# A decoder layer in float32: q and k of the first two head pairs by seven block products instead of direct projections

## The chip, the core and the metric

One core of a Trainium2 chip runs the whole program. The metric is the device time in microseconds (us) of one execution, as the median of several. TensorE is PE in the profile (PEld its weight loads), VectorE is DVE, ScalarE is ACT, GpSimd is POOL, and SP issues almost all DMAs, in the order in which they stand on its queue.

## The reference

A decoder layer over four batches of 1024 tokens and 512 features: attention, a gated causal convolution and a quantised feed-forward layer, each with a residual and a norm. The change concerns only the projections at the start. q, k and v are each two linear layers in a row:

```python
q = _lin(_lin(x, wq_w, wq_b), vq_w, vq_b)
k = _lin(_lin(x, wk_w, wk_b), vk_w, vk_b)
v = _lin(_lin(x, wv_w, wv_b), vv_w, vv_b)
...
scores = jnp.einsum('cbqh,cbkh->cbqk', q, k) / scale
attn = jax.nn.softmax(scores, axis=-1)
o = jnp.einsum('cbqk,cbkh->cbqh', attn, v)
```

There are 32 heads of 16 features. Everything is float32.

## The kernel before

**Set-up.** The two weights of each projection are multiplied once on TensorE ("fold", line 384 for q and k), so that q, k and v become one product each with x. The two biases are folded too: VectorE multiplies rows of the second weight by the first bias (line 367), reduces them (line 368) and adds the second bias (line 369). V's folded bias, `b_vc`, is a column over partitions but is needed as a row on all partitions, so it goes out to DRAM and comes back broadcast (lines 800 and 801). V's own fold (`fold_v`, line 546) is done in eight pieces of 256 columns.

**Units and pairs.** Attention runs in 32 units of four heads. A pair is two units of one batch and has 128 features of q and of k. The features of a pair are computed into a pack with 128 partitions, and `to_quadrants` (line 398) then moves 16 rows of each head to the start of a quadrant of 32 partitions, by four DMAs for each unit and each of q and k. Four units' worth of quadrants exist (`q_ts`, `k_ts`).

**Two ways to compute q and k.** `project` (line 407) computes one pair directly: six pieces of 176 or 160 columns, each four input tiles by four column groups of TensorE (`by_quarters`). It serves pairs 0 and 1. All later pairs are made two at a time by `product` (line 482): the two pairs and the two halves of the tokens form a 2 by 2 block matrix, the two halves of the input features another, and seven block products (in Winograd's form of Strassen's method) replace eight. The seven need sums of blocks of the weights (`sum_w`, four additions of 128 × 256 on POOL) and of x (`sums_of_x`, four of 128 × 1024 on POOL, of which the last overwrites one block of x). The result of each product is copied from PSUM by ScalarE and added to the right blocks by POOL; products 2, 3 and 4 go through one of four scratch rows ("rooms"). Product 7 uses `b_diff`, the difference of two pairs' biases.

**The order around the change** is written out by hand, engine by engine. Ahead of the first scores: two pieces of q of pair 0, then the other ten pieces of pair 0, with `to_quadrants` after q's last and after k's last, then five of V's eight folds, three sums of x, the sums of w for pair 2, and V's bias through DRAM. Then step u = −1 computes the row maxima of unit 0 (`nat`, line 603; half of them, "nats", use slots of the pool `ps_st`, which has four), and between groups of them a list of filling work: the last three folds, the 12 pieces of pair 1, V's block sums and the fourth sum of x, V's products for batch 0, and the first six parts of pairs 2 and 3. V's first products are added to `v_sb` by VectorE straight from PSUM, with V's bias row; V's later ones are copied by ScalarE to the rooms and added by POOL. x of batch 1 is loaded at the start of this step. After it the units of attention follow, always with the maxima of the next unit between the scores of this one.

Of the kernel before, what the change touches and what calls it, by code (L numbers as in the profile page):

```python
# [8 lines left out]
F32 = mybir.dt.float32  # L9
AF = mybir.ActivationFunctionType  # L10
ALU = mybir.AluOpType
# [41 lines left out]
def by_quarters(nc, pt, lhsT, rhs, tiles=FT):  # L53


    for f in range(tiles):
        for j in range(4):
            r = slice(32 * j, 32 * j + 32)
            nc.tensor.matmul(pt[r, :], lhsT(f)[:, r], rhs(f), start=f == 0, stop=f == tiles - 1)  # L59
# [193 lines left out]
def attention(ctx, tc, a, attn_d, ident, shared, hand):  # L253
# [7 lines left out]
    b_k = const.tile([P, FT], F32, tag="b_k", name="b_k")  # L261
    b_v = shared.tile([P, D], F32, tag="b_f", name="b_v")

    def big_slot(b, name):
        return shared.tile([P, NT * (D + 1)], F32, tag=f"big{b % 2}", name=name)

# [81 lines left out]
    for which, (w, v, dst) in enumerate((("wq", "vq", b_q), ("wk", "vk", b_k), ("wv", "vv", None))):  # L348
        w_n = sp.tile([P, FT, D], F32, tag="w_n", name=f"w_n{which}")
        v_t = sp.tile([P, FT, D], F32, tag="v_t", name=f"v_t{which}")  # L350
        for m in range(FT):
            rows = slice(m * P, (m + 1) * P)
            nc.sync.dma_start(w_n[:, m, :], a[f"{w}_w"][rows, :])

            (nc.scalar if which == 0 else nc.sync).dma_start(v_t[:, m, :], a[f"{v}_wT"][rows, :])
        v_n = w_v if which == 2 else rows_of_v[:, which * FT : (which + 1) * FT, :]
        w_b = sp.tile([P, D], F32, tag="w_b", name=f"w_b{which}")
        v_b = sp.tile([P, FT], F32, tag="v_bc", name=f"v_b{which}")
        if dst is None:
            dst = sp.tile([P, FT], F32, tag="b_vc", bufs=1, name="b_vc")  # L360

        def bias(w=w, v=v, dst=dst, v_n=v_n, w_b=w_b, v_b=v_b):

            nc.sync.dma_start(v_n, a[f"{v}_w"].rearrange("(t p) m -> p t m", p=P))
            nc.sync.dma_start(w_b, a[f"{w}_b"].partition_broadcast(P))
            nc.sync.dma_start(v_b, a[f"{v}_bc"])
            nc.vector.tensor_mul(v_n, v_n, w_b.unsqueeze(1).to_broadcast([P, FT, D]))
            nc.vector.tensor_reduce(dst, v_n, AX.X, ALU.add)
            nc.vector.tensor_add(dst, dst, v_b)

        if which == 2:
            bias()
            b_d = dpool.tile([D], F32, tag="b_v", bufs=1, name="b_vd")
            b_vc = dst
            break
        if which == 1:
            xts[0] = load_x(0)
        bias()
        w_d = (w_q, w_k)[which]

        pts = [ps.tile([P, D], F32, tag="ps", name=f"fold{which}_{f}") for f in range(FT)]
        for m in range(FT):
            for f in range(FT):
                nc.tensor.matmul(  # L384
                    pts[f], w_n[:, m, f * P : (f + 1) * P], v_t[:, m, :], start=m == 0, stop=m == FT - 1
                )
        for f in range(FT):
            if f % 2:
                nc.scalar.copy(w_d[:, f, :], pts[f])
            else:  # L390
                nc.vector.tensor_copy(w_d[:, f, :], pts[f])
# [6 lines left out]
    def to_quadrants(u, which, packed):  # L398
# [4 lines left out]
            nc.sync.dma_start(dst[32 * j : 32 * j + HD, :], packed[h * HD : (h + 1) * HD, :])  # L403
        if which == 0 and u >= 4:
            nc.sync.dma_start(dst[HD::32, :], dst[HD + 1 :: 32, :])

    def project(p, which, t0, n, packed, pool=None):

        b, gg = divmod(p, 4)
        w, bias = ((w_q, b_q), (w_k, b_k))[which]  # L410
        cols = slice(t0, t0 + n)
        pt = (pool or ps_st).tile([P, QW], F32, tag="ps" if pool else "st", name=f"proj{p}_{which}_{t0}")
        by_quarters(nc, pt[:, 0:n], lambda f: w[:, f, gg * P : (gg + 1) * P], lambda f: xts[b][:, f, cols])
        nc.scalar.activation(packed[:, cols], pt[:, 0:n], AF.Identity, bias=bias[:, gg : gg + 1], scale=1.0)
        if t0 + n == S:
            to_quadrants(2 * p, which, packed)
            to_quadrants(2 * p + 1, which, packed)

    def qk_pieces(p, which):

        parts = [(0, 176), (176, 176), (352, 176), (528, 176), (704, 160), (864, 160)]
        return [
            lambda pool=None, part=part: project(p, which, *part, packs[p][:, which, :], pool) for part in parts
        ]

# [51 lines left out]
        rooms.append(rooms.pop(0))  # L479
        return rooms[-1]  # L480

    def product(p, which, i, t0, n):

        b, gg = divmod(p, 4)
        left, right = operands(i, blocks_of_w(p, which), [w_sums[:, which, k, :, :] for k in range(4)], b)
        cols = slice(t0, t0 + n)
        pt = ps_st.tile([P, 512], F32, tag="st", name=f"part{i}_{p}_{which}_{t0}")[:, 0:n]
        by_quarters(nc, pt, lambda k: left[:, k, :], lambda k: right[:, k, cols], 2)
        c11, c12, c21, c22 = (
            packs[which][:, o, 512 * t + t0 : 512 * t + t0 + n] for o in range(2) for t in range(2)  # L490
        )
        if i in (2, 3, 4):
            dst = room()[:, 0:n]
        else:
            dst = {1: c11, 5: c22, 6: c12, 7: c21}[i]
        if i in (1, 7):
            bias = (b_q, b_k)[which][:, gg : gg + 1] if i == 1 else b_diff[:, which, gg // 2 : gg // 2 + 1]
            nc.scalar.activation(dst, pt, AF.Identity, bias=bias, scale=1.0)
        else:
            nc.scalar.copy(dst, pt)  # L500
        add = nc.gpsimd.tensor_add
        if i == 6:
            add(c12, c12, c11)
        elif i == 2:
            add(c11, c11, dst)
        elif i == 7:
            add(c21, c21, c12)
        elif i == 5:
            add(c12, c12, c22)
            add(c22, c22, c21)  # L510
        elif i == 3:
            add(c12, c12, dst)
        elif i == 4:
            nc.gpsimd.tensor_sub(c21, c21, dst)

    due = {}

    def products(p, which):


        rows = [(2 * p - 3, 2), (2 * p - 2, 2), (2 * p - 1, 2), (2 * p, 2)]
        if which == 1:
            rows = [(2 * p - 2, 22), (2 * p - 2, 26), (2 * p - 1, 4), (2 * p, 4)]
        for n, when in enumerate(rows):
            due.setdefault(when, []).append(lambda n=n: to_quadrants(2 * p + n, which, packs[which][:, n // 2, :]))
        return [
            [
                lambda part=part: product(p, which, *part)
                for part in parts
            ]  # L530
            for parts in (
                [(1, 0, 256), (1, 256, 256), (6, 0, 256), (6, 256, 256), (2, 0, 256), (2, 256, 256)],
                [(7, 0, 512), (5, 0, 512), (3, 0, 256), (3, 256, 256), (4, 0, 256), (4, 256, 256)],
            )
        ]


    early = qk_pieces(0, 0)
    for piece in early[:2]:
        piece(early_ps)  # L540
    setup_ps.close()

    ps_st = ctx.enter_context(tc.tile_pool(name="ps_st", bufs=4, space=PSUM))
# [243 lines left out]
    ]  # L787

    folds = [lambda f=f, half=half: fold_v(f, half) for f in range(FT) for half in range(2)]

    b_diff = const.tile([P, 2, 2], F32, tag="b_diff", name="b_diff")
    for which, bias in enumerate((b_q, b_k)):
        nc.vector.tensor_tensor(b_diff[:, which, :], bias[:, 1::2], bias[:, 0::2], ALU.subtract)
    for piece in early[2:] + qk_pieces(0, 1) + folds[:5]:
        piece()
    late_sum = sums_of_x(0)
    for work in late_sum[:3]:
        work()
    sum_w(2, 0)
    nc.sync.dma_start(b_d.rearrange("(t p) -> p t", p=P), b_vc)  # L800
    nc.sync.dma_start(b_v, b_d.partition_broadcast(P))

    for u in range(-1, NU):
        fill = []
# [12 lines left out]
        if u == -1:  # L817
            def sums():
                sum_blocks(v_blocks, v_sums)
                late_sum[3]()  # L820

            vs = v_parts[:6] + [[(i, t), (j, t)] for t in range(4) for i, j in ((6, 7), (5, 4))]
            fill = folds[5:] + qk_pieces(1, 0) + qk_pieces(1, 1) + [sums] + [
                lambda part=part: v_products(0, part) for part in vs
            ] + fill
        elif units[u][0] + 1 < B:
            b, g = units[u][0] + 1, units[u][1]
            v1, v2 = (lambda n=n, b=b: v_products(b, v_parts[n]) for n in (2 * g, 2 * g + 1))

            fill = {  # L830
                0: fill[:2] + [v1] + fill[2:4] + [v2] + fill[4:],
                1: [v1, v2] + fill,
                2: fill[:2] + [v1] + fill[2:4] + [v2] + fill[4:],
                3: fill + [v1, v2],
            }[w]
# [445 lines left out]
```

## Time and profile before

| what | us |
|---|---|
| median of 4 runs (2400.5 to 2401.67) | 2401.46 |
| the profiled execution, as timed | 2401.24 |
| its span, first to last instruction | 2399.3 |
| folds of q and k on TensorE | 5.48 to 33.38 |
| q and k of pair 0 | 33.38 to 47.30 |
| five of V's folds | 47.30 to 56.05 |
| first score product (maxima of unit 0) | 56.05 |
| first scores for the exponentials | 127.99 |

In the page, the first part gives busy times of the engines and their share of the span, and the fourth part the chain of work that ended last, followed back from the end. In a line of a timeline the first number is the start, the second the time taken (of a merged group: from its first start to its last end), then engine, line, operation, output from inputs, shape and number of records, and in brackets the idle time ahead of it and what ended it. A float32 matmul leaves two records. Matmuls overlap, so a group's time is read best from one start to the next.

### The profile page before, as it was taken

How to read it: one execution, taken by the hardware profiler on the slowest of the kernel's cores; microseconds unless marked ns; L12 is line 12 of the kernel's file. 1: busy time of each engine (PE TensorE's matmuls, PEld its weight loads, DVE VectorE, ACT ScalarE, POOL GpSimd, SP SyncE). 2: the span in 40 equal slices, each digit the busy share in tenths (PEclk: the TensorE clock that was granted, in tenths of full speed). 3: DMA queues.
4: the chain of work that ended last, by engine and by line, in shares of the span. 5: the costliest groups of instructions: out<-in, count | busy, mean ns of one | idle time of the engine just before them, and what ended most of it. 6: DMA issues, size and time to landing. Idle time of an engine off the chain costs nothing.

```text
span 2399.3 us, 70081 instructions
## 1 busy us (share of the span) xinstructions
PE 2391.9 (100%) x30124; PEld 1617.0 (67%) x30124; DVE 1724.3 (72%) x2153; ACT 1361.3 (57%) x2693; POOL 713.6 (30%) x728
## 2 busy tenths in 40 slices
PE   9999999999999999999999999999999999999999
PEld 6566666666666666666666666666666799747994
DVE  3667777777777777777777777777777477868678
ACT  1166666666666666666666666666666723411333
POOL 4332322212223322222322212211110268422761
PEclk9999999999999999999999999999999999999999
DMA  6200112011001110110111012202300242160311
GB/s 224 60 2 17 27 25 56 17 30 25 18 17 30 21 52 21 30 21 17 31 21 22 17 30 77 63 17 50 93 12 13 82 150 89 67 232 18 124 36 70
DMA packets 80838, 121.43 MB, mean 51 GB/s; under 512 B 39072, under 2 KB 39328, under 8 KB 80528
## 3 DMA queue, kind: packets, MB, share of 16 engines
q1 hardware_dynamic: 79808, 115.77, 17.1%
q8 instruction: 237, 3.88, 0.7%
q10 hardware_dynamic: 720, 1.18, 0.1%
q14 instruction: 73, 0.60, 0.1%
HBM read 80.77 MB, written 18.35 MB: 41 GB/s over the span
## 4 chain that ended last, share of the span: by engine, by line
PE 99%; POOL 0%; DVE 0%; ACT 0%; DMA 0%; issue 0%; SPq 0%; DVEq 0%; ACTq 0%; POOLq 0%
PE nat L616 22%; PE av L712 20%; PE st L686 19%; PE part L59 8%; PE pc L1018 6%; PE pa L1018 6%; PE pf L1102 5%; PE v L59 4%; PE po L59 2%; PE po L242 2%; PE proj L59 1%; PE fold L384 1%; PE tr L1094 1%; PE fold L59 1%; PE nats L616 0%; POOL v_sb L588 0%
## 5 line engine op out<-in xcount | busy, mean ns | idle before, releaser
L632 DVE TENSOR_REDUCE mx<-nat 128x2 f32<-128x1024 f32 x1008 | 1187.9, 1220 | 436.2 <-PE st L686 401.7
L697 ACT ACTIVATE at<-st 128x512 f32<-128x512 f32 x2016 | 1042.6, 602 | 477.7 <-PE st L686 467.6
L616 PE MATMUL nat<-qk 32*128 32x512 f32 x4032 | 1011.5, 614 | 0.5 <-DVE mx L632 0.5
L686 PE MATMUL st<-qk 32*128 32x256 f32 x8064 | 1001.6, 387 | 0.0
L686 PEld LDWEIGHTS st<-qk 32*128 32x128 f32 x8064 | 691.4, 184 | 43.2 <-issue 1.2
L712 PE MATMUL av<-at,v_sb 128*32 128x256 f32 x8192 | 497.7, 382 | 0.3 <-ACT at L697 0.3
L616 PEld LDWEIGHTS nat<-qk 32*128 32x128 f32 x4032 | 343.7, 184 | 220.5 <-DVE mx L632 134.1
L712 PEld LDWEIGHTS av<-at,v_sb 128*32 128x32 f32 x8192 | 241.5, 109 | 220.5 <-ACT at L697 88.4
L759 POOL TENSOR_TENSOR o_n<-o_sb,rbc 128x512 f32<-128x512 f32 x64 | 95.8, 1518 | 226.6 <-DMA rbc<-rec_d 150.1
L1018 PE MATMUL pa<-xf,w 128*128 128x171 f32 x1024 | 159.8, 308 | 0.0
L1018 PE MATMUL pc<-xf,w 128*128 128x171 f32 x1024 | 159.7, 308 | 0.0
L1018 PEld LDWEIGHTS pc<-xf,w 128*128 128x128 f32 x1024 | 152.0, 189 | 0.9 <-issue 0.9
L1018 PEld LDWEIGHTS pa<-xf,w 128*128 128x128 f32 x1024 | 152.0, 189 | 0.0
L1029 ACT ACTIVATE u<-u,b_c 128x512 f32<-128x512 f32 x64 | 46.1, 721 | 158.8 <-DVE u L1028 158.8
L1102 PE MATMUL pf<-w_f,xq_t 128*128 128x512 f32 (+1 forms) x264 | 114.8, 579 | 0.0
L171 POOL TENSOR_TENSOR w<-w 128x512 f32<-128x512 f32 x64 | 81.4, 1305 | 95.4 <-DMA w<-in_conv_wT 63.5
L725 DVE TENSOR_TENSOR o_sb<-av,o_sb 128x256 f32<-128x256 f32 x128 | 54.4, 425 | 68.3 <-PE av L712 67.8
L723 ACT COPY o_sb<-av 128x256 f32<-128x256 f32 x128 | 48.0, 375 | 77.7 <-PE av L712 64.5
L588 POOL TENSOR_TENSOR v_sb<-v_sb,extra 128x256 f32<-128x256 f32 x68 | 44.7, 686 | 139.7 <-ACT extra L572 139.7
L588 POOL TENSOR_TENSOR v_sb<-v_sb,rooms 128x256 f32<-128x256 f32 x56 | 36.8, 686 | 155.1 <-ACT rooms L572 155.1
L1102 PEld LDWEIGHTS pf<-w_f,xq_t 128*128 128x128 f32 x264 | 47.9, 190 | 45.8 <-issue 45.4
L1025 DVE SCALAR_TENSOR_TENSOR u<-pa,u 128x342 f32<-128x342 f32 x64 | 40.6, 635 | 50.5 <-PE pa L1018 48.0
(172 smaller groups left out, 2039.9 us busy)
## 6 DMA issues: line engine op xcount, KB each, us to landing
w<-in_conv_wT SPq DMA_DIRECT2D x32, 512.0 KB
u<-in_ctx SPq DMA_DIRECT2D x16, 1024.0 KB
xT<-in_xT SPq DMA_DIRECT2D x16, 512.0 KB
qk<-qk SPq DMA_DIRECT2D x128, 64.0 KB
qk<-extra SPq DMA_DIRECT2D x128, 64.0 KB
rbc<-rec_d SPq DMA_DIRECT2D x128, 64.0 KB
attn<-o_n SPq DMA_DIRECT2D x256, 32.0 KB
big<-attn SPq DMA_DIRECT2D x4, 2048.0 KB
```

Source lines behind the costliest of these rows:

```text
L59: nc.tensor.matmul(pt[r, :], lhsT(f)[:, r], rhs(f), start=f == 0, stop=f == tiles - 1)
L171: self.nc.gpsimd.tensor_tensor(w[:, i, tap, :], w[:, i, 0, :], w[:, i, 1, :], op)
L588: add(c, c, x)
L616: nc.tensor.matmul(pts[n], q_ts[u % 4][r : r + 32, qt * P : (qt + 1) * P], k_ts[u % 4][r : r + 32, kh * 512 : kh * 512 + 512], start=True, ...
L632: nc.vector.tensor_reduce(mxs[u][:, qt, 2 * pair : 2 * pair + 2, kh], pt, AX.X, ALU.max, negate=True)
L686: nc.tensor.matmul(st[:, k * QW : k * QW + QW], k_ts[u % 4][r : r + 32, kt * P : (kt + 1) * P], q_ts[u % 4][r : r + 32, qq * QW : qq * QW ...
L697: nc.scalar.activation(at, st, AF.Exp, scale=0.25)
L712: nc.tensor.matmul(av[32 * j : 32 * j + 32, :], v_sb[b % 2][:, kt, c * VW : c * VW + 32], ats[u, 2 * i + n // 2, j][:, n % 2 * QW : n % 2 ...
L725: nc.vector.tensor_add(o, av, o)
L759: nc.gpsimd.tensor_mul(o_n[:, :, half * 256 : half * 256 + 256], o_sb[:, cols].rearrange("p (s e) -> p e s", e=2), rbc[:, cols].rearrange( ...
L1018: nc.tensor.matmul(pt, w[:, i, tap, o : o + P], xf[:, tap, i, :], start=i == 0, stop=i == FT - 1)
L1102: nc.tensor.matmul(pt, xq_ts[b, t][:, f, :], hand.w_f[:, f, cols], start=f == 0, stop=f == FT - 1)
```

## The change

Pairs 0 and 1 are now made together by the seven products, first q, then k, all ahead of the first scores; `project` and `qk_pieces` are gone. The sums of x (all four) and the sums of w for pairs 0 and 1 come first on POOL, q's before the first product, k's after the second part. The sums of w for pair 2 move from the set-up to the place in step u = −1 where V's block sums are made. Of V's folds three stay ahead of the first scores and five go between them. `to_quadrants` moves q of units 0 and 1 after the tenth part and of units 2 and 3 after the twelfth, and k's likewise: 32 transfers ahead of the first scores on SP's queue, where 16 stood, and none for pair 1 later. The two DMAs of V's bias now stand ahead of them. `b_diff` is computed within each bias.

```diff
-        def bias(w=w, v=v, dst=dst, v_n=v_n, w_b=w_b, v_b=v_b):
+        def bias(w=w, v=v, dst=dst, v_n=v_n, w_b=w_b, v_b=v_b, which=which):
...
             nc.vector.tensor_add(dst, dst, v_b)
+            if which < 2:
+                nc.vector.tensor_tensor(b_diff[:, which, :], dst[:, 1::2], dst[:, 0::2], ALU.subtract)
...
-    def product(p, which, i, t0, n):
+    def product(p, which, i, t0, n, pool=None):
...
+    parts_of_two = (
+        [(1, 0, 256), (1, 256, 256), (6, 0, 256), (6, 256, 256), (2, 0, 256), (2, 256, 256)],
+        [(7, 0, 512), (5, 0, 512), (3, 0, 256), (3, 256, 256), (4, 0, 256), (4, 256, 256)],
+    )
...
-    early = qk_pieces(0, 0)
-    for piece in early[:2]:
-        piece(early_ps)
+    for work in sums_of_x(0):
+        work()
+    sum_w(0, 0)
+    for t0 in (0, 256):
+        product(0, 0, 1, t0, 256, early_ps)
     setup_ps.close()
...
-    b_diff = const.tile([P, 2, 2], F32, tag="b_diff", name="b_diff")
-    for which, bias in enumerate((b_q, b_k)):
-        nc.vector.tensor_tensor(b_diff[:, which, :], bias[:, 1::2], bias[:, 0::2], ALU.subtract)
-    for piece in early[2:] + qk_pieces(0, 1) + folds[:5]:
-        piece()
-    late_sum = sums_of_x(0)
-    for work in late_sum[:3]:
-        work()
-    sum_w(2, 0)
     nc.sync.dma_start(b_d.rearrange("(t p) -> p t", p=P), b_vc)
     nc.sync.dma_start(b_v, b_d.partition_broadcast(P))
+
+    for which in range(2):
+        for n, part in enumerate(parts_of_two[0] + parts_of_two[1]):
+            if which == 0 and n < 2:
+                continue
+            if which == 0 and n == 2:
+                sum_w(0, 1)
+            product(0, which, *part)
+            if n in (9, 11):
+                for u in (n - 9, n - 8):
+                    to_quadrants(u, which, packs[which][:, n // 10, :])
+    for piece in folds[:3]:
+        piece()
...
             def sums():
                 sum_blocks(v_blocks, v_sums)
-                late_sum[3]()
+                sum_w(2, 0)
...
-            fill = folds[5:] + qk_pieces(1, 0) + qk_pieces(1, 1) + [sums] + [
+            fill = folds[3:] + [sums] + [
```

More of the change, by code (lines that the diff above doesn't have):

```diff
@@ L262, in attention @@
     b_v = shared.tile([P, D], F32, tag="b_f", name="b_v")
+    b_diff = const.tile([P, 2, 2], F32, tag="b_diff", name="b_diff")
     def big_slot(b, name):
@@ L405, in to_quadrants @@
             nc.sync.dma_start(dst[HD::32, :], dst[HD + 1 :: 32, :])
[L407 to L424, printed above, removed]
     def blocks_of_x(b):
@@ L486, in product @@
         cols = slice(t0, t0 + n)
-        pt = ps_st.tile([P, 512], F32, tag="st", name=f"part{i}_{p}_{which}_{t0}")[:, 0:n]
+        pt = (pool or ps_st).tile([P, 512], F32, tag="ps" if pool else "st", name=f"part{i}_{p}_{which}_{t0}")[:, 0:n]
         by_quarters(nc, pt, lambda k: left[:, k, :], lambda k: right[:, k, cols], 2)
@@ L525, in products @@
             due.setdefault(when, []).append(lambda n=n: to_quadrants(2 * p + n, which, packs[which][:, n // 2, :]))
[L526 to L535, printed above, removed]
-    early = qk_pieces(0, 0)
-    for piece in early[:2]:
-        piece(early_ps)
+        return [[lambda part=part: product(p, which, *part) for part in parts] for parts in parts_of_two]
+    for work in sums_of_x(0):
[3 more added lines that the diff above has]
+        product(0, 0, 1, t0, 256, early_ps)
     setup_ps.close()
```

## The prediction

> **What bounds the kernel now.** I read the page's busy times and chain first, then the granted clock by stretch, then the order of each engine up to the first unit of attention, because the change moves nothing behind it.
>
> ```profile
> PE 2391.9 (100%) x30124; PEld 1617.0 (67%) x30124; DVE 1724.3 (72%) x2153; ACT 1361.3 (57%) x2693; POOL 713.6 (30%) x728
> ...
> PE 99%; POOL 0%; DVE 0%; ACT 0%; DMA 0%; issue 0%; SPq 0%; DVEq 0%; ACTq 0%; POOLq 0%
> ```
>
> TensorE carries 99% of the chain that ended last, so work taken from TensorE shortens the span unless a new wait takes its place. The stretches by time (columns: stretch, length, busy time and records of PE, PEld, DVE, ACT, POOL, granted clock, DMA share, GB/s):
>
> ```profile
> 33.38:47.30 13.92, 13.92 (x385) 12.51 (x388) 4.89 (x6) 5.03 (x12) 0.00 (x0) 1.00 0.24 44
> 47.30:56.05 8.75, 8.75 (x168) 5.07 (x157) 0.00 (x0) 1.88 (x5) 0.00 (x0) 1.00 0.47 72
> 56.05:127.99 71.94, 71.67 (x1157) 39.75 (x1153) 45.95 (x72) 13.83 (x37) 29.41 (x40) 1.00 0.20 50
> ```
>
> First: the q and k of pair 0, 12 projection pieces, with POOL and almost the whole SP queue free. Second: five pieces of V's fold, which cover the transfers of k's rows. Third: the maxima of unit 0 (line 616) with everything else, up to the first exponentials' scores. TensorE is busy throughout, clock 1.00. In the third stretch there is one wait that the engine's busy time hides in part: three pairs of score products take 1.92 us elsewhere (56.05 to 57.97, 63.28 to 65.20) but 3.22 us from 116.23 to 119.45, so 1.3 us go to a slot that ScalarE and POOL free late.
>
> **What it takes from TensorE.** Removed: 24 projection pieces (12 of pair 0 ahead of the first scores, 12 of pair 1 between them). 12 cost 13.92, so 24 cost 27.84 us. Added: for q and for k seven products of 512 columns, 28 halves of 256 columns with eight matmuls each. V's products have the same shape, and their groups of eight start 0.865 us apart:
>
> ```profile
> 102.82 1.05 PE L59 MATMUL v<-v_sums,xT 128*32 128x256 f32 x16
> 103.68 1.05 PE L59 MATMUL v<-x_sums,x_sums 128*32 128x256 f32 x16
> 104.55 1.05 PE L59 MATMUL v<-w_v,x_sums 128*32 128x256 f32 x16
> ```
>
> 28 × 0.865 = 24.2 us, so TensorE loses 3.6 us of work. Five folds took 8.75 us; the three now left ahead of the first scores take 5.25. The first score product is therefore due at 33.38 + 24.2 + 5.25 = 62.85.
>
> **The sums on POOL.** Three sums of x stand there today, then the sums of w for pair 2:
>
> ```profile
> 25.27 2.00 POOL L446 TENSOR_TENSOR x_sums<-x_sums,xT 128x1024 f32<-128x1024 f32 x1
> 27.22 2.77 POOL L463 TENSOR_TENSOR w_sums<-w_qk 128x256 f32<-128x256 f32 x1
> 30.07 0.73 POOL L464 TENSOR_TENSOR w_sums<-w_sums,w_qk 128x256 f32<-128x256 f32 x1
> ```
> ```profile
> 26.19 3.22 DVE L367 TENSOR_TENSOR rows_of_v<-rows_of_v,w_b 128x2048 f32<-128x2048 f32 x1 [5.32 <-DMA w_b<-in_wk_b]
> ...
> 35.63 2.29 DVE L367 TENSOR_TENSOR w_v<-w_v,w_b 128x2048 f32<-128x2048 f32 x1 [2.25 <-DMA w_b<-in_wv_b]
> ...
> 40.28 0.16 DVE L369 TENSOR_TENSOR b_vc<-b_vc,v_b 128x4 f32<-128x4 f32 x1
> ```
>
> A sum of 0.73 took 2.77 beside VectorE's bias multiply, so the two exclude each other and cost POOL 2.04. The fourth sum of x (2.35 at 85.03 today) now comes at 27.22: 27.22 + 2.04 + 2.35 = 31.6, then four sums of w for q by 0.7: the second, which the second product needs, at 33.0, the last at 34.5. TensorE asks at 33.38 + 2 × 0.865 = 35.1: hidden, with 2.1 us of margin. The four sums for k follow, meet the multiply of 35.63 (2.29), and end near 39.7; k asks only after 45.5. They delay POOL's first additions by about 3 us. POOL's additions cost 9.7 us for each of q and k (eight of 0.8, three of 1.3) against 12.1 of TensorE, so POOL has caught up when k's last ones come. The first scratch row asked for again (q's fourth product, at 43.8) was freed near 42.8. I count nothing; without the margins it would be the third rival.
>
> **The wait that can replace it: k's rows.** Today k's rows leave from 47.97 and TensorE arrives at 56.05. Now 16 transfers of q (units 0 to 3) and the trip of V's bias through DRAM stand on SP's queue ahead of k's first, and the trip holds everything behind it:
>
> ```profile
> 41.06 12.28 SPq L403 DMA_DIRECT2D qk<-qk  x16
> 53.44 0.53 SPq L800 DMA_DIRECT2D b_vd<-b_vc  x1
> 61.31 0.33 SPq L801 DMA_DIRECT2D b_v<-b_vd  x1
> ...
> 85.95 6.30 SPq L403 DMA_DIRECT2D qk<-extra  x8
> ```
>
> Bias column ready at 40.44 today; VectorE may wait for one POOL sum, so 40.9. The trip took 7.87 (53.44 to 61.31), the second issue 0.38: q's rows start at 49.1, though POOL has them near 48. The 16 issues above are two batches of 5.80 (41.06 to 46.86) and 5.37 (47.97 to 53.34), 0.70 us each. 16 × 0.70 puts k's first at 60.3. POOL's own end for k: TensorE ends the fifth product at 62.85 − 5.25 − 4 × 0.865 = 54.1, copy 0.7, two additions 2.65 (158.26 to about 160.9), two of the third product 1.6: 59.1, just before. So SP decides. k's fourth transfer is issued at 60.3 + 3 × 0.70 = 62.4 and lands 1.9 us later (line 656 issued at 92.35 and its dependent left at 94.31): 64.3. TensorE wants it at 62.85 + 0.64: a stall of 0.8 us. Bounds: spacing 0.64, the shortest in those batches, makes POOL the later one, the fourth lands at 62.9, no stall; 0.79 (8 in 6.30) starts k at 61.7, lands 66.0, 2.5 us. I take 0.8, nearest to the 16 back-to-back issues.
>
> The Trainium skill, "DMA: Bandwidth & Descriptors", section on issuing engines, says that the time a sequencer needs to start a transfer is usually small beside the transfer. Here the row speaks otherwise: 0.70 us an issue while the DMA share was 0.24 and 0.47. By the rule this stall would be zero and the gain the full 3.6.
>
> V's bias itself, issued at 48.75 rather than 61.31, is wanted by VectorE near 78 (62.85, four groups of scores 6.8, five folds 8.75): hidden. Left behind 32 transfers (32 × 0.70 from 48, plus 7.9) it would have been asked for at 78.3 and been late. Moving the two small differences of b_q and b_k earlier adds 0.15 us twice to VectorE, before copies that k alone needs. x of batch 1 is issued near 71.5 rather than 61.69, wanted at 132.
>
> **Between the first scores.** Of the 71.94, 13.92 was pair 1; two folds (3.5) come in: 61.5 with the old 1.3 of waiting. VectorE's direct additions (4 × 1.33 and 2 × 0.7) now lie in four groups, 20.7 us against 23.3 of TensorE. V's tail: POOL worked from 104.38 to 124.99 for it, 20.6 us, against some 19.6 of TensorE over the same pieces. The sums of pair 2, 2.9 us, stand behind V's sums near 84 to 87; they are wanted after 110. I carry the 1.3 unchanged; bounds 0 and twice that.
>
> **Sum.** −3.6 + 0.8 + 0 = −2.8. On the profiled execution: span 2399.3 − 2.8 = 2396.5, and the 1.9 around it (2401.24 less 2399.3) gives 2398.4; the median 2401.46 lies 0.2 above that run: 2398.7. The bounds together: −3.6 − 1.3 = −4.9 and −3.6 + 2.5 + 1.3 = +0.2.
>
> **Rivals.**
> Everything hidden: spacing at 0.64 and the 1.3 gone, since the order of V's pieces around the scores changes. For: POOL and SP meet almost at 59. Against: POOL's 20.6 us for V is unchanged. −3.6 − 0.8 = −4.4 with part of the 1.3: 2397.1.
> Slower, by SP's queue: k's rows stand behind 16 issues, and one long issue in two makes the mean spacing 1.0 (single ones took 1.34 and 1.64; the 15 around 74.93 waited between batches). k starts at 65.1, the fourth lands at 70.0, a stall of 6.5: +2.9, 2404.4. It decides from 49.1 + 19 × s + 1.9 = 67.1, s = 0.85. Against: no batch of eight was over 0.79.
> The Trainium skill, "TensorE: Matmul & The Clock Gate", section on why this matters for kernels, warns that an idle gap above about 3 us halves the clock. No row here has a gap over 1.1 us, all clocks are 1.00; the rule would add some 2 us to this rival alone.
> POOL late: the multiply blocks it twice, rooms come late, products wait 2 us in sum. −3.6 + 0.8 + 2 = −0.8: 2400.7. For: margins are 2.1 and 1.0. Against: POOL's additions are lighter than TensorE's products.
> That it does not do what it says: the built order has the 28 halves, the bias ahead of the rows, and no projection left; at most the bias was hidden anyway, which costs the 1.1 us from 48 to 49.1 already in the sum.
>
> **How the numbers follow.** Forecast 0.62, its own range 2397.4 to 2400.4. Everything hidden 0.14, POOL late 0.12, SP's queue 0.12. Range 2396.9 to 2402.2: it leaves out most of the slower rival and the last of the hidden one. 0.2% is 4.8 us, about what a measurement of this kernel can tell from no change: below 2396.7 only if every bound falls well, 0.05; above 2406.3 only the slower rival with spacing over 1.1 or a cold clock, 0.06; within, 0.89.
>
> **What would show it.** The products from 33.4 to 57.6 without idle time (3.6 right; gaps ahead of the second product or at a reused room: POOL late). On SP, V's second bias issue near 48.8, q's 16 issues 0.70 apart, k's first near 60.3. TensorE idle before the third and fourth score products near 0.8, released by the DMA of k. Scores of unit 1 starting near 125.2 instead of 127.99, and the same distance kept to the end. The prediction falls if the stall there is over 3 us, or if the distance changes behind the first unit.

## The result and the profile after

The changed kernel takes 2405.22 us (median of 42 runs, 2402.17 to 2407.34) against 2401.45 before (60 runs): a ratio of 1.0016, 95% interval 1.0011 to 1.0020. The forecast was 2398.7, 2.8 us faster; it became 3.8 us slower. The profiled execution has a span of 2402.4 (2404.43 us as timed) against 2399.3, so the traces differ by 3.1.

The page's busy times and chain after the change:

```profile
PE 2393.0 (100%) x29740; PEld 1611.2 (67%) x29740; DVE 1726.8 (72%) x2153; ACT 1362.0 (57%) x2693; POOL 739.9 (31%) x758
...
PE 97%; DMA 2%; DVE 0%; SPq 0%; ACT 0%; issue 0%; DVEq 0%
```

TensorE has 384 fewer records than before (29740 against 30124), yet more busy time (2393.0 against 2391.9), and DMA has come into the chain. Fewer matmuls that take longer in sum point to the clock. The stretches around the first score product (columns as in the prediction; the seventh value is the granted clock):

```profile
63.40:65.60 2.20, 0.03 (x1) 0.00 (x0) 0.00 (x0) 0.37 (x1) 0.00 (x0) 1.00 0.60 97
65.60:67.00 1.40, 1.38 (x5) 0.71 (x6) 0.00 (x0) 0.00 (x0) 0.00 (x0) 0.99 0.66 108
67.00:70.40 3.40, 3.40 (x21) 1.30 (x24) 2.70 (x4) 0.00 (x0) 0.00 (x0) 0.50 0.65 105
70.40:72.00 1.60, 1.60 (x36) 0.92 (x32) 0.98 (x1) 0.08 (x1) 0.00 (x0) 1.00 0.59 100
```

TensorE is idle for 2.2 us, starts again, and from 67.0 to 70.4 runs at half its clock. In its timeline the first three pairs of score products take 3.88 us (65.62 to 69.50), and the two folds behind them 4.00 (to 73.50). In the kernel before the same pairs took 1.92 (56.05 to 57.97, the last two lines here), and two folds take 3.6 at full clock (75.41 to 79.00). So some 2.4 us are lost beside the wait.

```profile
65.62 1.92 PE L599 MATMUL nat<-qk 32*128 32x512 f32 x4 [2.19 <-DMA qk<-extra]
...
69.50 4.07 PE L59 MATMUL fold<-v_t,w_n 128*32 128x256 f32 x64
73.50 0.70 PE L599 MATMUL nats<-qk 32*128 32x512 f32 x2
```
```profile
56.05 0.70 PE L616 MATMUL nat<-qk 32*128 32x512 f32 x2
...
57.97 5.39 PE L59 MATMUL fold<-v_t,w_n 128*32 128x256 f32 x96
```

What the first score product waits for is a transfer of k's rows. SP's queue, and below it POOL's last additions to k:

```profile
41.37 0.38 SPq L773 DMA_DIRECT2D b_vd<-b_vc  x1
50.26 0.32 SPq L774 DMA_DIRECT2D b_v<-b_vd  x1
50.67 12.43 SPq L407 DMA_DIRECT2D qk<-qk  x16
63.21 10.99 SPq L407 DMA_DIRECT2D qk<-extra  x16
```
```profile
58.17 1.43 POOL L497 TENSOR_TENSOR extra<-extra 128x256 f32<-128x256 f32 x2
59.55 1.42 POOL L499 TENSOR_TENSOR extra<-extra,rooms 128x256 f32<-128x256 f32 x2
```

k's rows of units 0 and 1 are complete on POOL at 59.6 (the end of the first of its two lines; the second belongs to units 2 and 3), but SP comes to them only at 63.21, behind V's bias (8.9 us from write to read) and 16 transfers of q. They land at 65.6; the folds ended at 63.4.

First scores for the exponentials start at 130.37 instead of 127.99, so 2.4 of the 3.1 us are there by then; the other 0.7 come in small steps over the rest of the span. The median lies 0.8 above the profiled execution as timed: of the 42 runs, the 17 with a mean granted clock of 0.998 have a median of 2405.66, the 24 with 0.999 (the profiled one among them) 2404.90.

### The profile page after: what moved, and what is told of

Its sections match the earlier page's. It is cut to its first block, busy times and chain, and to the rows that moved or that the text cites. A ratio compares the mean times of both kernels' runs of the same rounds, so it can differ in the third digit from the quotient of the medians.

```text
span 2402.4 us, 69362 instructions
## 1 busy us (share of the span) xinstructions
PE 2393.0 (100%) x29740; PEld 1611.2 (67%) x29740; DVE 1726.8 (72%) x2153; ACT 1362.0 (57%) x2693; POOL 739.9 (31%) x758
## 4 chain that ended last, share of the span: by engine, by line
PE 97%; DMA 2%; DVE 0%; SPq 0%; ACT 0%; issue 0%; DVEq 0%
PE nat L599 22%; PE av L695 20%; PE st L669 19%; PE part L59 8%; PE pc L1004 6%; PE pa L1004 6%; PE pf L1088 5%; PE v L59 4%; PE po L59 2%; PE po L242 2%; PE nats L599 1%; PE tr L1080 1%; PE fold L388 1%; PE fold L59 0%; DMA b_vd<-b_vc 0%; DMA w_b<-in_wv_b 0%
```

## The experiments

Two questions were open: whether the half clock belongs to the gap or to something else in the change, and what makes k's rows late. Theory A in the expectations is the reading above. Each median stands beside the runs of the kernel before on the same chip, with the difference of the two and the 95% interval of the ratio. Since the kernel before itself differs by up to 0.5 us from one set of runs to another, kernels of different sets are compared by their differences.

| kernel | us | before | difference | ratio, 95% | profiled span, clock |
|---|---|---|---|---|---|
| the changed kernel | 2405.22 | 2401.45 | +3.8 | 1.0011 to 1.0020 | 2402.4, 0.999 |
| five folds ahead | 2399.34 | 2400.96 | −1.6 | 0.9984 to 1.0002 | 2396.1, 1.000 |
| bias read later | 2399.88 | 2400.96 | −1.1 | 0.9987 to 1.0004 | 2397.5, 1.000 |
| gap filled | 2402.74 | 2400.96 | +1.8 | 0.9999 to 1.0017 | 2400.4, 1.000 |
| before, no fold ahead | 2407.15 | 2400.96 | +6.2 | 1.0016 to 1.0036 | 2405.7, 0.998 |
| before, one fold ahead | 2404.39 | 2401.07 | +3.3 | 1.0006 to 1.0024 | 2401.8, 0.999 |
| short gap | 2403.54 | 2401.21 | +2.3 | 1.0002 to 1.0020 | 2399.2, 1.000 |
| bias behind | 2407.08 | 2401.21 | +5.9 | 1.0014 to 1.0034 | 2405.0, 0.998 |
| k first | 2399.05 | 2401.21 | −2.2 | 0.9983 to 1.0000 | 2398.3, 0.999 |
| all orders | 2399.39 | 2401.21 | −1.8 | 0.9984 to 1.0001 | 2396.9, 1.000 |
| k first, four folds | 2398.91 | 2401.07 | −2.2 | 0.9983 to 1.0000 | 2397.3, 1.000 |

### The gap and the clock

**The gap filled with work that nobody reads.** Nothing arrives earlier; only the idle time goes.

```diff
     for piece in folds[:3]:
         piece()
+    for n in (512, 512, 256):
+        pt = ps_st.tile([P, 512], F32, tag="st", name=f"cover{n}")[:, 0:n]
+        nc.tensor.matmul(pt, w_n[:, 0, 0:P], v_t[:, 0, 0:n], start=True, stop=True)
```

> The changed kernel with three matmuls that nobody reads (128x128 by 512, 512 and 256 columns, 2.1 us) after the third fold, so that TensorE works through the wait for k's rows; nothing arrives earlier. Theory A: the wait itself stays, but without idle time the clock is not halved: 2405.2 - 2.4 = 2402.8 us, clock 1.00 from 65 to 71 us. Rival B (the drop isn't due to the gap): 2405.2 us, clock near 0.5 from 67 to 70 us as before.

Measured 2402.74, as theory A said (2402.8), all 11 runs between 2402.17 and 2403.79. The same stretch of its trace:

```profile
63.40:65.80 2.40, 2.40 (x8) 1.06 (x7) 0.00 (x0) 0.37 (x1) 0.00 (x0) 1.00 0.67 108
65.80:68.30 2.50, 2.50 (x13) 1.03 (x12) 1.15 (x2) 0.00 (x0) 0.00 (x0) 1.00 0.63 105
68.30:71.90 3.60, 3.60 (x67) 1.98 (x64) 2.40 (x4) 0.37 (x1) 0.00 (x0) 1.00 0.56 91
```

The first score product starts at 65.79, as late as in the changed kernel, but the clock stays at 1.00, and three pairs take 2.5 us, two folds 3.6. The half clock thus follows from the idle time. By the differences to the kernel before it costs 3.8 − 1.8 = 2.0 us, as much as the two profiled spans differ (2402.4 and 2400.4). The two 95% intervals overlap, but 41 of the changed kernel's 42 runs lie above all 11 of these, and the trace shows the clock itself. Of the 2.4 us lost beside the wait 1.8 are the clock's; the other 0.6 stay at full clock too, most likely because k's rows land one after another.

**Five folds ahead of the first scores.**

```diff
-    for piece in folds[:3]:
+    for piece in folds[:5]:
...
-            fill = folds[3:] + [sums] + [
+            fill = folds[5:] + [sums] + [
```

> The changed kernel with five of V's folds ahead of the first scores instead of three; two folds less between them. Theory A (the first score product waits 2.2 us for k's rows, and the idle time then halves the granted clock for some 3.5 us, another 2.4 us): 3.5 us of folds cover the wait, no idle time there, clock 1.00 throughout, 2405.2 - 4.6 = 2400.6 us. Rival B (the slow stretch from 65.6 to 70 us belongs to the sparse score products themselves, not to the gap): only the 2.2 us of waiting go, 2403.0 us, and the clock still drops.

Measured 2399.34, 1.3 below theory A's 2400.6 and far from rival B's 2403.0. No wait for k's rows is left in the trace, the first score product starts at 65.86 right behind the fifth fold, clock 1.00:

```profile
57.11 8.82 PE L59 MATMUL fold<-v_t,w_n 128*32 128x256 f32 x160
65.86 0.70 PE L599 MATMUL nat<-qk 32*128 32x512 f32 x2
```

Against the kernel before, the three steps are +3.8, +1.8 without the half clock, −1.6 without the wait.

**The kernel before with a gap.** The converse: the old way to compute q and k, with all folds behind the first maxima (`folds[:5]` becomes an empty list, `folds[5:]` becomes `folds`). The work is the same, only its order differs.

> The kernel before the change with none of V's folds ahead of the first scores (all eight between them): TensorE comes to the first score product near 47.3 us and k's first row lands near 49.9. No work is added. Theory A: a gap of about 2.6 us and then a halved clock for some 3 us: 2401.5 + 2.6 + 2.4 = 2406.5 us. Rival B: the gap alone, 2404.1 us, clock 1.00.

Measured 2407.15, 6.2 above the kernel before; expected were 5.0. The half clock lasted twice as long as in the changed kernel:

```profile
47.80:50.70 2.90, 0.00 (x0) 0.01 (x1) 0.00 (x0) 0.39 (x1) 0.00 (x0) 1.00 0.50 81
50.70:51.10 0.40, 0.39 (x1) 0.28 (x2) 0.00 (x0) 0.00 (x0) 0.00 (x0) 0.97 0.74 123
51.10:57.90 6.80, 6.80 (x40) 3.23 (x42) 3.55 (x4) 0.00 (x0) 0.00 (x0) 0.50 0.35 52
57.90:60.00 2.10, 2.10 (x44) 1.20 (x40) 0.00 (x0) 0.37 (x1) 0.00 (x0) 1.00 0.00 0
```

A gap does this without any of the change's products in the kernel.

**How short a gap is enough.** One unread matmul of 512 columns after the third fold in the changed kernel:

> The changed kernel with one unread matmul (128x128 by 512, 0.86 us) after the third fold: the arrival of k's rows unchanged, the gap about 1.3 us instead of 2.2. Theory A with a threshold between 1.3 and 2.2 us: clock 1.00, 2402.8 us as with the gap filled. Without a threshold in that range: the clock still halves for some 3.5 us, 2405.2 us.

Inconclusive on the length of the gap. The runs spread from 2401.09 to 2406.66; the profiled one is the fastest, its rows came early, its gap was 0.47 us and its clock 1.00.

```profile
64.27 1.65 PE L599 MATMUL nat<-qk 32*128 32x512 f32 x4 [0.47 <-DMA qk<-extra]
```
```profile
64.00:66.00 2.00, 1.73 (x5) 0.88 (x6) 0.00 (x0) 0.00 (x0) 0.00 (x0) 1.00 0.63 105
```

Time and clock go together over the 11 runs: the four fastest (up to 2402.78) have a mean granted clock of 1.000, the seven from 2403.42 on 0.999 or less (which also 3 of 31 runs of the kernel before have). So the half clock probably came in some executions and not in others; no trace of a slower one shows it, nor how long its gap was. Then one fold ahead in the kernel before (`folds[:1]` and `folds[1:]`):

> The kernel before the change with one of V's folds ahead of the first scores instead of five: TensorE comes there 1.75 us later than without any, so the gap of 2.96 us falls to about 1.2 us. If the half clock has a threshold between 1.2 and 2.2 us of idle time: the gap alone, at most 2402.7 us, clock 1.00. If a gap of 1.2 us is enough: 2405 us or more in most executions, with some 3.4 or 6.8 us at half clock.

Measured 2404.39, all 11 runs at or above 2403.63: a loss of 3.3 us by the medians, though the gap was short. That lies between the two times that were expected (at most 2402.7, or 2405 and more); the trace decides, with 3.5 us at half clock.

```profile
48.40:49.90 1.50, 0.06 (x4) 0.00 (x0) 0.00 (x0) 0.37 (x1) 0.00 (x0) 1.00 0.40 63
49.90:52.00 2.10, 2.06 (x5) 0.88 (x6) 0.00 (x0) 0.00 (x0) 0.00 (x0) 1.00 0.61 100
52.00:55.50 3.50, 3.50 (x20) 1.13 (x22) 3.04 (x4) 0.00 (x0) 0.00 (x0) 0.51 0.43 60
```

1.5 us without work were enough, with a sparse stretch behind them: from 49.9 to 52.0 only five records stand where the filled kernel has 13 in 2.5 us, and one weight load there waits 0.66 us for a row. "Busy" there is time in which a few matmuls are under way. Whether the idle 1.5 us alone would do it is not separated from that.

### What makes k's rows late

**The bias read back behind k's first rows**, its write left where the change put it:

```diff
     nc.sync.dma_start(b_d.rearrange("(t p) -> p t", p=P), b_vc)
-    nc.sync.dma_start(b_v, b_d.partition_broadcast(P))
...
                     to_quadrants(u, which, packs[which][:, n // 10, :])
+                if which == 1 and n == 9:
+                    nc.sync.dma_start(b_v, b_d.partition_broadcast(P))
```

> The changed kernel with the write of V's bias column to DRAM where it is, but its read back moved behind the rows of k of units 0 and 1, so that q's rows don't wait for the write to land. Theory A (SP's queue, held 8.9 us by the bias, sets when k's rows leave): q's rows start near 47.4 us instead of 50.7, k's near 60 instead of 63.2, the idle time ahead of the first score product falls to under 0.5 us, the clock stays at 1.00: 2400.6 us. Rival C (POOL's additions set it, k's pack is only ready near 60.2): k's rows land at least 2 us after the folds end, a gap of 1 us or more stays: 2403 us or more.

Measured 2399.88. SP's queue now:

```profile
41.67 0.38 SPq L773 DMA_DIRECT2D b_vd<-b_vc  x1
48.38 10.52 SPq L407 DMA_DIRECT2D qk<-qk  x16
59.26 5.71 SPq L407 DMA_DIRECT2D qk<-extra  x8
65.01 0.58 SPq L786 DMA_DIRECT2D b_v<-b_vd  x1
```

q's rows leave when POOL has them, k's at 59.26 instead of 63.21; the first score product follows the third fold without a wait. Rival C, that POOL's additions cause the gap, falls.

**k of units 0 and 1 ahead of q of units 2 and 3**, with the bias as in the change:

```diff
-                for u in (n - 9, n - 8):
-                    to_quadrants(u, which, packs[which][:, n // 10, :])
+                if which == 1 and n == 11:
+                    for u in (2, 3):
+                        to_quadrants(u, 1, packs[1][:, 1, :])
+                elif n == 9:
+                    for u in (0, 1):
+                        to_quadrants(u, which, packs[which][:, 0, :])
+                    if which == 1:
+                        for u in (2, 3):
+                            to_quadrants(u, 0, packs[0][:, 1, :])
```

> The changed kernel with the rows of q of units 2 and 3 moved behind those of k of units 0 and 1; bias and folds unchanged. Theory A (k waits behind 16 issues): the queue is free at 56 us, k's rows leave when POOL has them, near 60, and land from 62.3 to 64.3; gap under 0.7 us, no half clock, 2400.5 us. Rival C (POOL's additions are the limit): gap of 1 us or more, 2403 us.

Measured 2399.05. The queue stands free after eight transfers, and k's rows leave at 60.18:

```profile
51.05 0.32 SPq L774 DMA_DIRECT2D b_v<-b_vd  x1
51.47 5.71 SPq L407 DMA_DIRECT2D qk<-qk  x8
60.18 4.96 SPq L407 DMA_DIRECT2D qk<-extra  x8
65.18 5.86 SPq L407 DMA_DIRECT2D qk<-qk  x8
```

So neither part of the queue's load makes k late alone: taking away either the trip of V's bias or eight of q's 16 issues is enough to be rid of the gap.

**The bias behind all 32 transfers**, where the old order would have it (both of its DMAs moved behind the loop over the products):

> The changed kernel with both DMAs of V's bias behind all 32 transfers of rows, where the order before the change had them. Theory A: q's rows leave near 47.5 us, k's near 60, no gap ahead of the first score product and clock 1.00 there, but the bias is written only near 71 us and lands broadcast near 81; V's first additions, wanted near 78, wait some 3 us on VectorE, and x of batch 1 leaves near 80. Maxima behind them are late, TensorE waits 0 to 2 us: 2400 to 2402.5 us. Rival D (V's bias late costs as much as the gap did: a second idle time and a second half clock near 80 us): 2404 us or more.

Measured 2407.08; rival D was right, theory A's price of 0 to 2 us was wrong. The first gap is gone, but VectorE stands still for 5.63 us for the bias, the score products behind wait 4.4 us for a slot in PSUM that V's products hold, and the clock halves there, from 85.7 to 92.5:

```profile
84.73 0.42 DVE L562 TENSOR_TENSOR v_sb<-v,b_v 128x256 f32<-128x256 f32 x1 [5.63 <-DMA b_v<-b_vd]
```
```profile
82.00:84.00 2.00, 0.00 (x0) 0.00 (x0) 0.00 (x0) 0.00 (x0) 2.00 (x3) 1.00 0.46 184
84.00:86.00 2.00, 0.00 (x0) 0.00 (x0) 1.27 (x4) 0.00 (x0) 1.92 (x4) 0.92 1.04 422
86.00:88.00 2.00, 1.71 (x2) 0.50 (x2) 2.00 (x4) 0.00 (x0) 0.47 (x1) 0.50 1.01 412
...
92.00:94.00 2.00, 2.00 (x36) 0.88 (x28) 1.39 (x4) 0.00 (x0) 0.00 (x0) 0.88 0.00 0
```

So the bias can't simply go last; what costs in the change is that the queue waits for the bias ahead of the rows.

### Versions

Five folds, the bias read later and k first together:

> The changed kernel with five folds ahead of the first scores, the bias read back behind k's first rows, and q of units 2 and 3 behind them too. If the gap was all that was wrong, there is no gap to remove beyond the five folds: the same as five folds alone, 2399.3 us in the runs shared with it. Rival: a shorter first wait lets V's bias or x of batch 1 come earlier too, 2398.5 us or less.

2399.39, 1.8 us below the kernel before, as five folds alone (1.6). And k first with four folds:

> The changed kernel with k of units 0 and 1 ahead of q of units 2 and 3 on SP's queue, and four folds ahead of the first scores. Theory A: with k first there was no gap left at three folds (2399.05 us), so a fourth only moves work: 2399.0 us within 0.5. Rival: rows of k still late by some tenths in the unprofiled executions, and a fourth fold saves them: 2398.4 us or less.

2398.91, the lowest median measured, within what theory A said. It lies below the kernel before by 2.2 us (0.9992, the interval ends at 1.0000) and its slowest run (2399.72) lies below the fastest of the kernel before on the same chip (2400.1). The five versions without a gap (these two, five folds, the bias read later, k first) lie 1.1 to 2.2 us below the kernel before, with intervals that reach 1.0000 or beyond, and aren't told apart.

## The prediction, step by step

**3.6 us less work on TensorE: right.** In the kernel with the bias read later TensorE needs 29.45 us from the first product to the first score product (33.54 to 62.99), to the hundredth the 24.2 + 5.25 of the prediction. The profiled changed kernel took 30.36 for the same stretch. Nearly all of these 0.9 us stand between 48.6 and 51.2, with no wait of TensorE in the trace, and their cause is open. They did not make the first score product later, since k's rows landed later still.

**The sums on POOL hidden: right.** No product waited for one. The fourth sum of x took 4.40 us beside VectorE's multiply, as worked out.

**0.8 us of wait for k's rows: the mechanism right, the size too small.** The wait was expected ahead of the third and fourth score products, for k's fourth row; already the first product waited, 2.19 us, for the first row. The terms: bias column stored from 41.37 (forecast 40.9), its trip 8.89 us (7.87), 16 issues in 12.54 (11.2, at 0.78 each rather than 0.70), the first row landed 2.4 us after its issue (1.9, which had been read from a smaller transfer, 16 KB to DRAM). k's first issue came at 63.21 instead of 60.3. The spacing came out near the forecast's upper bound (0.79), and the trip was a term without bounds. With the 0.6 us by which the rows behind the first are late, the stall is 2.8, just over the forecast's upper bound of 2.5. The Trainium skill, "DMA: Bandwidth & Descriptors", section on issuing engines, calls the time to start a DMA usually small beside the DMA itself. The trace differs: the 16 issues stood 0.78 us apart at a DMA share of 0.55 (50.67 to 63.21), and the queue set the time. Single issues took 0.51 to 1.70 us; why is not shown.

**What a gap costs beyond itself: the step that failed.** The sum priced the stall by its length alone, 0.8 us, and held no term for the clock behind it: the prediction wrote that an idle gap "above about 3 us" halves the clock and that this would add some 2 us to the slower rival alone. That figure came from the Trainium skill, "TensorE: Matmul & The Clock Gate", section on why this matters for kernels, which advises against idle gaps above about 3 us between bursts of matmuls. No row of the trace before could show it, since TensorE's longest wait there was 1.1 us, at the very start. Here 2.2 us of idle time were followed by 3.4 us at half clock, and 1.5 us with sparse products behind them by 3.5 us in the kernel before with one fold, so the figure was too high for this kernel. By the differences to the kernel before, the stall cost 5.4 us (+3.8 against −1.6 with five folds): 2.0 for the clock and 3.4 for the wait (2.8 in the trace), where the sum had 0.8. The gain of 3.6 was spent. The clock is not the whole miss: the filled kernel, at +1.8 without any half clock, is still 4.6 us above the forecast of −2.8. Of these, 2.6 are the longer wait, and 2.0 are lost even where there is no gap (−1.6 instead of −3.6).

**Nothing more lost between the first scores: 1 us or so too little.** The prediction has 61.5 us from the first score product to the first scores; the kernel with the bias read later, with no gap, took 62.94, k first 62.40. The old wait at 116 us (1.3) did go, but others came. Twice VectorE reaches maxima only behind V's direct additions, and four records that take 1.02 us elsewhere take 1.83 and 1.75. And the last group, eight records that took 1.07 in the kernel before (123.04 to 124.11), takes 2.10; two of its weight loads wait for VectorE's maxima (0.15 and 0.30 us). The prediction had set 20.7 us of VectorE against 23.3 of TensorE over these pieces; that sum says nothing of the order, and the order made the waits. In the changed kernel (the trace of k first has the same three):

```profile
85.47 1.83 PE L599 MATMUL nats<-qk 32*128 32x512 f32 x4
...
97.31 1.75 PE L599 MATMUL nats<-qk 32*128 32x512 f32 x4
...
125.54 0.70 PE L599 MATMUL nat<-qk 32*128 32x512 f32 x2
...
127.64 1.07 PE L59 MATMUL part<-x_sums,w_sums 128*32 128x256 f32 x16
```

**The same distance kept to the end: nearly.** It grows from 2.4 to 3.1 us in steps of 0.2 to 0.3; with five folds ahead it shrinks from −3.5 to −3.2, with steps at the same places. A distance that changes behind the first unit was one of the prediction's own signs of being wrong. The cause is open.

So without a gap the change is worth 1.1 to 2.2 us by the medians, not 3.6 and not 2.8: some 1 us goes between the first scores, most of it where VectorE is late, some 0.2 to 0.7 to the steps. The rival whose time came nearest was the slower one by SP's queue (2404.4), but by luck: its condition, a spacing of 0.85 us or more, did not come (0.78), and its wait was 6.5 us instead of 2.2. The half clock, which it did not count, brought the time near.

## What to carry to other kernels

When work is taken from the engine that bounds a kernel, ask what each thing that it used to cover now waits for, and price a new gap on TensorE with the slow clock behind it, not by its length alone. A DMA that waits for another to land holds everything behind it on its queue: issue the first half early and the second half behind the urgent transfers, and put the rows that are wanted first at the head. Independent work moved into a gap, as two folds here, saves the gap and the slow clock; matmuls that nobody reads save the slow clock alone (2.0 us here).

## What the hardware showed

The granted clock mostly fell to 0.50 not during the idle time but after work had resumed: 1.4 us after it in the changed kernel (work from 65.6, half clock from 67.0), 2.1 and 0.4 in the kernel before with one fold and with none; with the bias behind, at the end of the idle time. Counted from the end of the dense work, the drop came after nearly the same time in all four: 3.6 us (63.4 to 67.0), 3.6 (48.4 to 52.0), 3.3 (47.8 to 51.1) and 3.8 (81.9 to 85.7). With the short gap the stretch from dense work to dense work was only 3.45 us (63.80 to 67.25) in the profiled run, and the clock stayed at 1.00. This fits a clock that reacts to some 3.5 us of little work, idle or sparse; no run tests it by itself. The slow stretch lasted 3.4 to 3.5 us in the changed kernel and with one fold, and 6.8 with no fold and with the bias behind (85.7 to 92.5). A write of 512 floats as a column to DRAM took 7.9 to 8.9 us before the dependent read could be issued, with the DMA engines almost idle for most of it.
